# One token transfer of 256 KB in place of two of 128 KB in the spectral steps of a conv, attention and spectral-filter kernel

## The chip, the cores and the metric

The kernel runs on one core of one Trainium2 chip, as one launch. The metric is device microseconds for one execution; the time of a kernel is the median of several runs. A second figure, the span, is the time from the first to the last instruction of the one execution that the hardware profiler recorded.

## The reference, cut to what matters

The network has two images of 64 x 64 pixels and 128 channels (4096 tokens of 128 channels each). It normalises them, runs a convolutional self-attention block with four heads, then an attention of the tokens with themselves, and last a spectral layer. The change touches the spectral layer alone: a causal convolution of the tokens with 16 filters, each result multiplied by its own 128 x 128 matrix and summed.

```python
def _stu_conv(phi, u, n):
    Vf = jnp.fft.rfft(phi, n=n, axis=0)
    Uf_p = jnp.fft.rfft(u, n=n, axis=1)
    Uf_m = jnp.fft.rfft(u * sgn3, n=n, axis=1)
    U_plus = jnp.fft.irfft(Vf[None, :, :, None] * Uf_p[:, :, None, :], n=n, axis=1)[:, :sl]
    U_minus = jnp.fft.irfft(Vf[None, :, :, None] * Uf_m[:, :, None, :], n=n, axis=1)[:, :sl]
...
out = jnp.einsum('btkd,k,kde->bte', U_plus, s, Mpp)
out = out + jnp.einsum('btkd,k,kde->bte', U_minus, s, Mpm)
```

Here `btkd` are batch, time, filter and channel; the input is (2, 4096, 128) and there are K = 16 filters.

## The kernel before, in words

Up to about 1713 us the kernel does the first attention block, the second attention, and the preparation of the spectral layer. In that preparation the function `feed` transforms the tokens along one time index and writes them to DRAM as `rows16[b]`: float16, indexed by half (high and low part of the number), component, row, frequency and channel. The filters' tables lie in DRAM as `tables16`.

From there on the spectral layer runs in 64 steps, numbered by batch `b`, output parity `ro`, one of eight chunks of 16 frequencies `ch`, and stream `s`. A step has three parts.

- `fetch16(n)` brings the data of step `n` into SBUF. It is called for step `n + 2` at the head of step `n`. For each half of the chunk (8 frequencies) it issues two token transfers from GpSimd (L1213) and one table transfer of 1 MB from SyncE (L1222). A token transfer fills 64 partitions, one for each combination of half, component (2 x 2) and row (16), with one contiguous row of 8 frequencies x 128 channels, 2 KB. The two copies put the same data on partitions 0 to 63 and 64 to 127. In DRAM the source is a pattern of 4 blocks of 16 rows.
- `convolve16` multiplies on TensorE: 16 matmuls (L1606) with the tokens as weights and the tables as the moving operand, four for each of four windows `w`; windows 0 and 1 use the first half, 2 and 3 the second. ScalarE (L1613) and VectorE (L1614) split each result into two float16 parts.
- `mix16` multiplies these parts by the filters' matrices on TensorE, 48 matmuls (L1622). They are given out twelve at a time between the windows of the next step's `convolve16`.

The tiles have three turns: step `n` uses turn `n % 3` of `tokens_in` (a pair of tiles for each turn, one for each half) and of `tables_in` (the same). A fetch into a turn waits until the matmuls that read the old contents are done. The transfers and the spectral matmuls keep the order in which they are written (`ordered`). On the GpSimd queue a transfer also waits until the one eight places ahead of it has landed, because eight semaphores are used in turn there.

Other work goes beside the steps: `back` takes a finished quarter of the output, adds `base`, which it reads from DRAM with a transfer of 1 MB (`had`), and writes the result; in the first steps the rest of `feed` for the second batch is also on the GpSimd queue (`rows`, L1412 and L1413).

Of the kernel before, what the change touches and what calls it, by code (L numbers as in the profile page):

```python
# [13 lines left out]
F16 = mybir.dt.float16  # L14
# [8 lines left out]
P = 128  # L23
B, C, HH, WW = 2, 128, 64, 64
# [15 lines left out]
BP = NI // 2  # L40
# [7 lines left out]
NS = NF // NCH // 2  # L48
# [28 lines left out]
def conv_attn_hybrid(ctx: ExitStack, tc: tile.TileContext, io):  # L77
    nc = tc.nc
# [31 lines left out]
    def pool(stack, name, bufs=1, **kw):  # L110
        return stack.enter_context(tc.tile_pool(name=name, bufs=bufs, reuse_waits="tile", **kw))
# [5 lines left out]
    def chain(*parts):  # L117
        for p in parts:
            yield from p
# [589 lines left out]
    rows16 = [dram.tile([2, 2, DROWS, NF, C], F16, name=f"rows16_{b}") for b in range(B)]  # L709
# [44 lines left out]
    def network(layer0, in_halves):  # L754
        with ExitStack() as st:
            layers(st, layer0, in_halves)

    def layers(st, layer0, in_halves):
# [3 lines left out]
        tokens = [pool(st, f"tok{b}", side="right") for b in range(B)]  # L762
# [223 lines left out]
        def transform(p):  # L986

            fw = p.tile([P, 4, NF], F32, name="fw", bufs=1)
            aside.dma_start(fw, io["fw"])
            return fw  # L990
# [3 lines left out]
        if not in_halves:  # L994
            tokens_in = ffw.tile([P, 2, 2, WC // 2, C], F32, name="tokens_in")
# [53 lines left out]
        def rest16(p, steps):  # L1049
            wbr, top = chosen[:2]  # L1050
            ends = p.tile([P, NBR, P], F32, name="ends")
            aside.dma_start(ends, io["ends"].partition_broadcast(P))
            mu_raw = p.tile([P, NBR, NU, C], F32, name="mu_raw")
            aside.dma_start(mu_raw, io["mu"].rearrange("i n d e -> d i n e"))
            aside.dma_start(gw, io["gw16"])
            yield from steps
            weighted_sum(mask, ends, top)
            yield
            weighted_sum(mu, mu_raw, wbr)
            yield  # L1060
            nc.vector.scalar_tensor_tensor(
                gw, gw, OUT_SCALE, mask.unsqueeze(1).to_broadcast([P, 2, P]), ALU.mult, ALU.mult
            )
            yield
# [128 lines left out]
        def ordered(instruction):  # L1193
            return tc.keep_in_program_order(instruction)
# [4 lines left out]
        if in_halves:  # L1199
            tables_in, tokens_in = [], []  # L1200

        def fetch16(n, pieces=1):

            if n >= len(STEPS):
                return
            b, ro, ch, s = STEPS[n]
            row = FIRST[STREAM[ro, s]]
            for half in range(2):
                w0 = 2 * NS * ch + NS * half
                tt, ut = halves16(n)[half]  # L1210
                for copy in range(2):
                    ordered(
                        nc.gpsimd.dma_start(  # L1213
                            ut[64 * copy : 64 * copy + 64],
                            rows16[b].rearrange("h c r w d -> (h c) r w d")[:, row : row + BP, w0 : w0 + NS, :],
                        )
                    )
                own = tables16[s, w0 // NS]
                size = BP // pieces
                for part in range(pieces):  # L1220
                    ordered(
                        nc.sync.dma_start(  # L1222
                            tt[:, part * size : part * size + size],
                            bass.AP(
                                tensor=own.tensor,
                                offset=own.offset + part * size * NS * 2 * NK,
                                ap=[[NDI * NS * 2 * NK, 8], [NS * 2 * NK, BP], [1, size * NS * 2 * NK]],
                            ),
                        )
                    )  # L1230
                    yield

        def spaced(steps):
            for _ in steps:
                for _ in range(3):
                    yield

        def halves16(n):
            return list(zip(tables_in[n % 3], tokens_in[n % 3]))

        def attend16(b, p, beside, closed, drain=True):

# [217 lines left out]
        with ExitStack() as l1:  # L1460
            p1 = pool(l1, "l1")
            if not in_halves:
                lo.append(p1.tile([P, L], F32R, name="lo"))
            with ExitStack() as part:
                p = pool(part, "l1_a")
                gate = [0]

                def second_parts(n):
                    if n < NQ and not in_halves:
                        low = p.tile([P, 2, 512], F32, tag="low", name=f"low{n}")  # L1470
                        nc.sync.dma_start(low, lows[n].rearrange("n p c -> p n c"))
                        copy = nc.vector.tensor_copy(loT[0][:, bass.ts(n, 512)], low[:, 0])
                        if n == 0:
                            tc.keep_in_program_order(copy)
                        nc.vector.tensor_copy(lo[0][:, bass.ts(n, 512)], low[:, 1])

                def ready(i):
                    second_parts(i + 1)

                second_parts(0)  # L1480
                fw = None if in_halves else transform(p1)

                def closed(j):
                    gate[0] = j + 1

                y = [None]

                def stage(i, n):
                    y[0] = p.tile([P, 512], F32, tag="y", name=f"y1_{i}")
                    return y[0]  # L1490

                stats = LayerStats(p1, tok[1], "a1")
                second = normalise(1, stats, stage, gate)
                if in_halves:
                    steps = chain(left, rest16(p, stats.steps()), second)
                else:
                    steps = chain(left, stats.steps(), filters(p, fw), matrices(p), second)
                (attend16(0, p1, steps, closed) if in_halves else attend(0, p1, steps, closed, ready))
            right0.close()
            if in_halves:  # L1500
                early = pool(middle, "early", side="right")
                tables_early = [early.tile([P, BP, NS, 2 * NK], F16, name=f"tables_e{n}") for n in range(2)]
                tokens_in = [
                    [early.tile([P, NS, C], F16, name=f"tokens{turn}_{n}") for n in range(2)] for turn in range(3)
                ]
                tables_in.append(tables_early)
                late_pool = pool(right1, "late", 2, side="right")
                fw = transform(late_pool)
                banked = [bank]
                fed_to = [0]  # L1510
            if in_halves:
                mxr, mxl = mixing
            else:
                mxr, mxl = (x[0].rearrange("p (k s c) -> p k s c", k=NK, s=2) for x in (hiT, loT))
            with ExitStack() as part:
                p = pool(part, "l1_b", 2)
                fed = LayerStats(ffw, tok[1], "f1")

                def closed(j):
                    fed.take(range(4 * j, 4 * j + 4))  # L1520
                    fed.close(range(4 * j, 4 * j + 4))
                    own = slice(2 * j, 2 * j + 2)
                    m = p.tile([P, 2, 2, C], F32, tag="m", name=f"m{j}")
                    aside.dma_start(m, mx[own].rearrange("k p s c -> p k s c"))
                    nc.vector.tensor_copy(mxr[:, own], m)
                    nc.vector.tensor_tensor(mxl[:, own], m, mxr[:, own], ALU.subtract)
                    if in_halves:
                        fed_to[0] = j + 1

                if in_halves:  # L1530
                    ahead = spaced(fetch16(0, 4))
                    feed_1 = feed(1, late_pool, lambda name: banked[0](name), fw, fed, fed_to)
                    beside = chain(feed(0, late_pool, bank, fw), by_turns(ahead, feed_1))
                    attend16(1, p1, beside, closed, drain=False)
                    for _ in ahead:
                        pass
                else:
                    attend(1, p1, feed(0, p, bank, fw), closed)
# [12 lines left out]
        else:  # L1551
            tables_in = [
                px.tile([P, 2, WC // 2, 2 * BP * NK], F32, tag=f"b{n}", name=f"tables_in{n}") for n in range(2)
            ]
# [385 lines left out]
```

## Time and profile before

| | before |
|---|---|
| median of 3 runs | 2728.48 us |
| the three runs | 2701.92, 2728.48, 2751.97 us |
| profiled execution, its own time | 2752.85 us |
| its span | 2751.0 us |
| mean granted TensorE clock | 0.980 |
| TensorE busy (matmul) | 2585.8 us, 94% of the span |
| token transfers | 256 of 128 KB, median 27.7 us from issue to landing |
| first and last spectral matmul that reads tokens | 1713.1 and 2714.4 us |

How to read it: the page names an instruction by its line, its engine, its operation and its tiles, written `out<-in`. "PE cv L1606" is a matmul of line 1606 into tile `cv`. A DMA is named by its tiles; its time to landing runs from the issue by its engine to the last of its semaphore updates. Idle time of an engine is put down to what ended it. PE is TensorE, PEld its weight load, DVE VectorE, ACT ScalarE, POOL GpSimd, SP SyncE; a small q after an engine is its queue.

### The profile page before, as it was taken

The numbers are of one execution on the slowest core, as the hardware profiler recorded it, in microseconds if no ns is written. First come the engines' busy times: TensorE is split into PE (matmuls) and PEld (weight loads), VectorE is DVE, ScalarE is ACT, GpSimd is POOL, SyncE is SP. The second block draws the span as 40 slices with busy tenths as digits, with TensorE's granted clock in tenths as the row PEclk, the third lists the DMA queues.
The fourth block names the chain that finished last, engine by engine and source line by source line (L and its number), as shares of the span: only waits on it lengthen the run. The fifth ranks groups of instructions, "written<-read, shape, count | busy, mean of one in ns | idle before, by whom it ended". The sixth has DMA issues, their size and how long they took to land.

```text
span 2751.0 us, 32520 instructions
## 1 busy us (share of the span) xinstructions
PE 2585.8 (94%) x11955; PEld 1277.3 (46%) x11955; DVE 1671.0 (61%) x2946; ACT 1840.3 (67%) x2059; POOL 492.9 (18%) x792
## 2 busy tenths in 40 slices
PE   5999999999998989999989999988898989999998
PEld 3555555555544444444434444433353435445444
DVE  5256464246357426878876677756565656666664
ACT  4999999999998887666544554544454545555553
POOL 2022021012122401000233322311111111111110
PEclk9999999999999999999989999999999999999999
DMA  5122220012113504766366865665565666665661
GB/s 145 35 66 66 61 72 20 5 53 66 30 32 100 79 20 90 129 113 110 71 131 124 150 124 118 199 170 142 171 176 151 137 172 217 190 203 180 159 198 56
DMA packets 328874, 311.65 MB, mean 113 GB/s; under 512 B 276240, under 2 KB 278944, under 8 KB 312512
## 3 DMA queue, kind: packets, MB, share of 16 engines
q1 hardware_dynamic: 270480, 221.61, 31.6%
q0 software_dynamic: 56784, 85.44, 13.3%
q10 hardware_dynamic: 1440, 2.43, 0.3%
q8 instruction: 96, 1.57, 0.2%
q14 instruction: 74, 0.61, 0.1%
HBM read 212.27 MB, written 23.33 MB: 86 GB/s over the span
## 4 chain that ended last, share of the span: by engine, by line
PE 33%; DMA 13%; DVE 6%; issue 5%; ACT 1%; POOL 1%; SPq 0%; DVEq 0%; POOLq 0%; ACTq 0%
PE m L1622 17%; DMA tokens<-rows 10%; PE cv L1606 6%; PE od L1280 3%; PE oa L1280 3%; PE y L1252 3%; DMA eT<-pair 2%; DVE pair L1266 2%; DVE x L1614 1%; DVE both L1300 1%; PE bk L1740 1%; PE pf L1406 1%; ACT ey L1261 1%; PE ar L1388 1%; PE vt L1730 0%
## 5 line engine op out<-in xcount | busy, mean ns | idle before, releaser
L465 ACT ACTIVATE e<-s 128x1536 f16<-128x1536 f32 (+1 forms) x704 | 938.9, 1425 | 63.3 <-PE s L209 58.7
L1614 DVE TENSOR_TENSOR x<-cv,x 128x1024 f16<-128x1024 f32 x512 | 602.9, 1219 | 329.7 <-ACT x L1613 329.6
L1613 ACT CAST x<-cv 128x1024 f16<-128x1024 f32 x512 | 493.8, 1016 | 446.4 <-PE cv L1606 444.6
L1622 PE MATMUL m<-x,mxr 128*128 128x512 f16 x2048 | 624.4, 382 | 0.0
L209 PE MATMUL acc<-e,v 128*97 128x512 f16 x2048 | 562.1, 382 | 15.7 <-DVE accs L413 13.1
L209 PE MATMUL s<-qs,ks 128*128 128x512 f16 x2048 | 561.7, 382 | 7.3 <-ACT e L465 3.8
L1622 PE MATMUL m<-x,mxl 128*128 128x512 f16 x1024 | 393.5, 384 | 1.2 <-DVE oh L1629 1.2
L209 PEld LDWEIGHTS <-v 128*97 128x97 bf16 x2048 | 256.3, 125 | 230.4 <-issue 30.4
L1261 ACT ACTIVATE ey<-y,nshift 128x512 f32<-128x512 f32 x288 | 196.3, 688 | 195.3 <-PE y L1252 162.2
L1622 PEld LDWEIGHTS <-mxr 128*128 128x128 f16 x2048 | 201.7, 98 | 244.7 <-issue 7.4
L209 PEld LDWEIGHTS <-ks 128*128 128x128 f16 x2048 | 201.7, 100 | 230.8 <-issue 49.1
L1213 POOL DMA_DIRECT2D tokens<-rows x256 | 157.1, 614 | 742.7 <-DMA tokens<-rows 492.8
L1252 PE MATMUL y<-bothT 128*128 128x512 f16 x864 | 204.4, 383 | 3.1 <-ACT ey L1261 2.1
L1266 DVE TENSOR_TENSOR pair<-ey,pair 128x1024 f16<-128x1024 f32 x144 | 174.5, 1218 | 35.7 <-ACT pair L1265 35.1
L1280 PE MATMUL od<-pair,hi 128*128 128x512 f16 x576 | 185.3, 383 | 9.3 <-DVE oT L1292 5.8
L1300 DVE SCALAR_TENSOR_TENSOR both<-eT 128x512 f16<-128x512 f16 x224 | 153.7, 686 | 55.7 <-DMA eT<-pair 52.4
L1606 PEld LDWEIGHTS <-tokens 128*128 128x128 f16 x1024 | 98.6, 98 | 179.8 <-issue 49.8
L413 DVE COPY accs<-acc 97x512 f32<-97x512 f32 x64 | 44.1, 690 | 212.7 <-PE acc L209 212.6
L1622 PEld LDWEIGHTS <-mxl 128*128 128x128 f16 x1024 | 101.4, 99 | 128.9 <-issue 6.8
L1280 PEld LDWEIGHTS <-hi 128*128 128x128 f16 x1024 | 101.1, 99 | 125.6 <-issue 12.9
L1265 ACT CAST pair<-ey 128x1024 f16<-128x1024 f32 x144 | 150.6, 1046 | 4.6 <-DMA eT<-pair 2.2
L1280 PE MATMUL oa<-eT,hi 128*128 128x512 f16 x448 | 143.3, 381 | 0.0
(224 smaller groups left out, 2348.0 us busy)
## 6 DMA issues: line engine op xcount, KB each, us to landing
tables_a<-tables SPq DMA_DIRECT2D x42, 1024.0 KB
tables_b<-tables SPq DMA_DIRECT2D x42, 1024.0 KB
tables_e<-tables SPq DMA_DIRECT2D x42, 1024.0 KB
tokens<-rows POOLq DMA_DIRECT2D x256, 128.0 KB, 27.7
tab<-in_rot SPq DMA_DIRECT2D x32, 512.0 KB
rows<-uh POOLq DMA_DIRECT2D x128, 64.0 KB, 4.3
ks<-term POOLq DMA_DIRECT2D x112, 64.0 KB, 2.3
qs<-term POOLq DMA_DIRECT2D x112, 64.0 KB, 2.0
```

Of the source, the lines that this page charges most:

```text
L209: tc.keep_in_program_order(nc.tensor.matmul(*args, **kw))
L465: nc.scalar.activation(e[:, own, :], ps[:, own, :], AF.Exp, scale=SCORE_SCALE)
L1213: nc.gpsimd.dma_start(ut[64 * copy : 64 * copy + 64], rows16[b].rearrange("h c r w d -> (h c) r w d")[:, row : row + BP, w0 : w0 + NS, :],)
L1252: nc.tensor.matmul(ps[:, q, :], a[0][:, bass.ts(t, P)], c[0][:, bass.ts(i, 512)], start=(n == 0), stop=(n == 2),)
L1261: nc.scalar.activation(e[:, q, :], ps[:, q, :], AF.Exp, bias=nshift16, accum_out=den[:, t, i : i + 1])
L1266: nc.vector.tensor_tensor(pair[:, 1, own], e, pair[:, 0, own], ALU.subtract)
L1280: nc.tensor.matmul(acc, a[0][:, own], pair(m, t), start=(start and t == 0 and n == 0), stop=(stop and t == 3 and n == 2),)
L1300: nc.vector.scalar_tensor_tensor(both, eT[:, 0, :, u, :], 1.0, eT[:, 1, :, u, :], ALU.mult, ALU.add, accum_out=den[:, 4 * i + u, j : j + 1],)
L1606: ordered(nc.tensor.matmul(pu[:, h, :], ut[:, at, :], tt[:, :, at, :], start=True, stop=True))
L1613: nc.scalar.copy(hi, pur)
L1614: nc.vector.tensor_tensor(lo, pur, hi, ALU.subtract)
L1622: nc.tensor.matmul(acc, m, x, start=(s == 0 and i == 0), stop=(s == 1 and i == len(products) - 1))
```

## The change

The tokens of a step become one tile per turn, 16 frequencies wide (4 KB on each partition), and are brought by two transfers of 256 KB in place of four of 128 KB. The two copies on the partitions' halves remain. `halves16` hands out the two halves of the one tile as views, so the matmuls are the same. The two token transfers stand ahead of both table transfers of the step.

```diff
@@ fetch16
             row = FIRST[STREAM[ro, s]]
+            for copy in range(2):
+                ordered(
+                    nc.gpsimd.dma_start(
+                        tokens_in[n % 3][64 * copy : 64 * copy + 64],
+                        rows16[b].rearrange("h c r w d -> (h c) r w d")[
+                            :, row : row + BP, 2 * NS * ch : 2 * NS * ch + 2 * NS, :
+                        ],
+                    )
+                )
             for half in range(2):
                 w0 = 2 * NS * ch + NS * half
-                tt, ut = halves16(n)[half]
-                for copy in range(2):
-                    ordered(
-                        nc.gpsimd.dma_start(
-                            ut[64 * copy : 64 * copy + 64],
-                            rows16[b].rearrange("h c r w d -> (h c) r w d")[:, row : row + BP, w0 : w0 + NS, :],
-                        )
-                    )
+                tt = tables_in[n % 3][half]
                 own = tables16[s, w0 // NS]
...
         def halves16(n):
-            return list(zip(tables_in[n % 3], tokens_in[n % 3]))
+            return [(tt, tokens_in[n % 3][:, NS * h : NS * h + NS]) for h, tt in enumerate(tables_in[n % 3])]
...
                 tokens_in = [
-                    [early.tile([P, NS, C], F16, name=f"tokens{turn}_{n}") for n in range(2)] for turn in range(3)
+                    early.tile([P, 2 * NS, C], F16, name=f"tokens{turn}") for turn in range(3)
                 ]
```

## The prediction, made before the changed kernel ran

> **What bounds the kernel now.** I read the time first: the shown runs are 2701.92, 2728.48 and 2751.97 us. The profiled execution is one of the long ones: 2752.85 us with a span of 2751.0, so 1.85 us lie outside the span and it is 24.4 us above the median. Two per cent, about what a measurement of this kernel can tell from no change, is 55 us.
>
> Next the page. TensorE is busy for 94% of the span; then the chain, which names the transfer that the change touches:
>
> ```profile
> PE 2585.8 (94%) x11955; PEld 1277.3 (46%) x11955; DVE 1671.0 (61%) x2946; ACT 1840.3 (67%) x2059; POOL 492.9 (18%) x792
> ...
> PE 33%; DMA 13%; DVE 6%; issue 5%; ACT 1%; POOL 1%; SPq 0%; DVEq 0%; POOLq 0%; ACTq 0%
> PE m L1622 17%; DMA tokens<-rows 10%; PE cv L1606 6%; PE od L1280 3%; PE oa L1280 3%; PE y L1252 3%; DMA eT<-pair 2%; DVE pair L1266 2%; DVE x L1614 1%; DVE both L1300 1%; PE bk L1740 1%; PE pf L1406 1%; ACT ey L1261 1%; PE ar L1388 1%; PE vt L1730 0%
> ...
> tokens<-rows POOLq DMA_DIRECT2D x256, 128.0 KB, 27.7
> ```
>
> Ten per cent of the chain, some 289 us, is spent in flight of token transfers: 128 KB take 27.7 us to land. That is not what can be won, since the chain follows a transfer while TensorE works as well. What TensorE really loses is in the table by stretches; its columns are start and end, length, busy us (instructions) of PE, PEld, DVE, ACT and POOL, granted clock, DMA share, GB/s:
>
> ```profile
> 1713.00:1796.00 83.00, 78.86 (x331) 36.11 (x330) 59.95 (x86) 42.76 (x49) 30.88 (x46) 0.98 0.63 198
> 1796.00:1968.00 172.00, 147.71 (x645) 63.72 (x644) 96.58 (x84) 78.77 (x84) 25.54 (x41) 0.94 0.61 154
> 1968.00:2046.00 78.00, 77.51 (x399) 40.72 (x398) 53.43 (x48) 40.45 (x44) 12.99 (x22) 1.00 0.60 187
> 2046.00:2246.00 200.00, 175.08 (x786) 77.66 (x785) 115.92 (x101) 94.53 (x100) 29.33 (x47) 0.95 0.60 148
> ...
> 2354.00:2494.00 140.00, 139.02 (x642) 62.47 (x643) 96.05 (x84) 78.15 (x83) 25.10 (x41) 1.00 0.60 199
> ```
>
> So the 64 spectral steps have two starved stretches, 1796 to 1968 and 2046 to 2246. TensorE is idle 24.3 + 24.9 us there, and the clock that falls after each idle time costs 0.06 x 172 + 0.05 x 200 = 20 us more: 69 us is all that the tokens can give back in this execution. In the quick stretches a step takes 13.81 us (2118.84 to 2132.66 in the timeline), which is TensorE's own work. The waits, and the timeline where one ends, say who is late:
>
> ```profile
> PE cv L1606 <- DMA tokens<-rows: 20.1, 5, 11.5
> ...
> POOL tokens L1213 <- DMA tokens<-rows: 491.0, 160, 6.1
> POOL tokens L1213 <- PE cv L1606: 171.2, 40, 6.6
> ```
>
> ```profile
> 2102.48 1.89 PE L1606 MATMUL cv<-tables_b,tokens 128*128 128x512 f16 x4 [11.47 <-DMA tokens<-rows]
> ...
> 2116.72 1.22 POOL L1213 DMA_DIRECT2D tokens<-rows  x2 [5.57 <-PE cv L1606]
> ...
> 2118.84 1.03 PE L1606 MATMUL cv<-tables_e,tokens 128*128 128x512 f16 x4
> ...
> 2132.66 1.03 PE L1606 MATMUL cv<-tables_a,tokens 128*128 128x512 f16 x4
> ```
>
> POOL's 491 us are waits of a token transfer for the one eight transfers earlier on the same queue: at most eight are in flight, two steps' worth.
>
> **Why 128 KB take 27.7 us.** The trace's semaphore updates give it. Of the 16 increments of one token transfer eight come after 1.7 to 5.5 us and eight after 16 to 41 us. The packet records show why: table packets (8192 B) fly on at most eight engines at a time, and these eight are always occupied. Each token transfer leaves 32 packets of 4096 B, 16 semaphore writes of 4 B and 96 records of 8 B. If four engines carry data (8 packets each) the other twelve get 8 small fillers each, 12 x 8 = 96. So on every engine a token transfer is 8 packets and a semaphore write, 9 items, and on the eight table engines the items come out one for one with table packets (at 2126 us a filler each 0.63 us, behind a table packet of 0.63 us; in quick stretches behind one of 0.31).
>
> [...]
>
> **The change, part by part.**
>
> Issues: 128 fewer on POOL at 0.61 us, 78 us of POOL. POOL waits most of the time in this stage, so nothing on the path. TensorE, VectorE, ScalarE and SP keep their order.
>
> Queue limit: eight transfers are now four steps' worth and three buffers hold six, so the 491 us of POOL waits end. What limits the issue next is the buffer, that is `cv` on TensorE. By itself it is worth nothing, since the table engines' queue was never empty with eight in flight.
>
> Items: a row is now 4 KB, one packet. 16 packets (or fillers; I assume one for each packet as before) and one semaphore write make 17 items, two transfers a step: 34 in place of 4 x 9 = 36. The bytes are the same. In the starved stretches the token queue sets the pace, so 372 us x 2/36 = 20.7 us come back. The unknown here is the fillers. Lower bound of the cost: if they stay 8 per transfer, an engine has (17 + 3 x 9)/4 = 11 items a transfer, 22 a step. Upper bound: a row goes as two packets, 32 + 1 items a transfer and 66 a step, which I all but exclude, since the tables' rows of 8 KB go as one packet. I take 34.
>
> Deadline: before, the first half's tokens were due at the step's first `cv` and the second half's 6.9 us later; now the whole is due at the first. Likewise the buffer comes free as a whole at the last `cv`, three quarters into the step. Lead for the first half falls from 2.75 steps (38 us) to 2.25 (31 us). Where the queue sets the pace this costs at most 6.9 us once for a stretch, not for each step, since then transfer follows transfer: 13.8 us for two. In the quick stretch between them tokens gain more of a cushion: there 36 items took 13.5 us by the landings (0.375 each), so 34 take 12.8 against TensorE's 13.81; over the five steps 15 to 19 that is 3.5 us more than before. Net cost 10 us.
>
> Sum for the profiled execution: -20.7 + 10.3 = -10.4 us, so 2742.5 from 2752.85. The median run has 24.4 us less of stall, 45 of 69; the same share of the gain is 7 us: 2728.5 - 7 = 2721 us.
>
> **Rivals.**
>
> Nothing to see: landing is set by semaphore writes behind table packets whatever the transfer's size, and gain and cost cancel. For it: the two numbers are of one size. 2728 us.
>
> Tokens stop being the bound: fillers stay 8, 22 items a step. Then the tables are next. By the packet records they landed 19 us early at the end of the first starved stretch and 11 us at the end of the second, so 30 us of idle go and, at 20 us of clock to 49 of idle, 12 more: 42 in the profiled run, 27 in the median one: 2701 us. Against it: data packets and fillers were equal in number before.
>
> Slower: the one piece comes too late. Its place is the first `cv` of a step; its price is the landing less the lead. In quick stretches landings of 26 to 28 us fit into 31. In some 26 steps (5 to 14, 20 to 31, 37, 38, 52, 53; table packets take 0.45 us or more in most of them) landings are some 36 us; if the queue gets no faster, each waits 5 us where it now loses 69/26 = 2.7: 26 x 2.3 = 60 us, 2788 us. It decides from a landing of 31 us on. Against it: a paced queue costs the half step once.
>
> **How the numbers follow.** Forecast 0.42, nothing to see 0.20, tokens no longer the bound 0.18, slower 0.20. The range takes in most of both sides, 2688 to 2775; before's own runs spread over 50 us. Faster by over 2% (under 2674) would need nearly all 69 us gone: 0.05. Slower by over 2% (over 2783) is most of the last rival: 0.13. Within: 0.82.
>
> **What would show it.** Right: 128 token issues; POOL no longer waiting for token transfers; fillers of 4 B, 192 a transfer; landings of 25 to 35 us; starved stretches still there, at step starts alone, with some 60 us of idle and clock loss. Wrong: 96 fillers, landings under 15 us and no idle before `cv` (the second rival), or idle before the first `cv` of most steps (the last one).

## The result: 1% slower, and the profile after

| | before | after |
|---|---|---|
| median of 22 runs each, same chip | 2712.12 us | 2741.38 us |
| lowest and highest | 2689.75, 2758.07 | 2708.42, 2787.98 |
| profiled execution, its own time | 2752.85 us | 2726.16 us |
| its span | 2751.0 us | 2724.2 us |

The ratio after to before is 1.0096, with a 95% interval of 1.0069 to 1.0123: 26 us (0.0096 x 2712) more, where I had forecast 7 us less. Runs over 1.5% above the fastest of the same kernel are left out of this ratio and of all later ones. The two profiled executions must not be subtracted: the one of before is among its longest and the one of after is below its median. What they do show is which waits there are.

The page of after, its rows for busy time, the chain by engine, POOL's issues and the transfers (us to landing last):

```profile
PE 2578.6 (95%) x11955; PEld 1276.3 (47%) x11955; DVE 1670.5 (61%) x2946; ACT 1839.1 (68%) x2059; POOL 411.7 (15%) x664
...
q0 software_dynamic: 54736, 85.33, 13.7%
...
PE 41%; DVE 7%; issue 5%; DMA 5%; ACT 2%; POOL 1%; SPq 0%; DVEq 0%; POOLq 0%; ACTq 0%
...
L1210 POOL DMA_DIRECT2D tokens<-rows x128 | 77.1, 607 | 780.5 <-PE cv L1608 739.5
...
tokens<-rows POOLq DMA_DIRECT2D x128, 256.0 KB, 21.4
```

POOL is 81 us less busy, its 491 us of waits for older token transfers are gone, and a transfer lands 6 us sooner. The queue has 2048 packets less than the 56784 before: 64 steps x 32, which is 4 x (32 + 16 + 96) less 2 x (64 + 16 + 192). So the fillers are 192 a transfer, as assumed. TensorE still starves. The table by stretches (start and end, length, busy of PE, PEld, DVE, ACT, POOL, clock, DMA share, GB/s) and the waits of TensorE and POOL from 1690 us on:

```profile
1800.00:1900.00 100.00, 81.10 (x348) 35.04 (x347) 52.91 (x46) 41.74 (x44) 6.74 (x12) 0.91 0.60 146
1900.00:2200.00 300.00, 293.93 (x1399) 138.72 (x1398) 200.57 (x175) 161.49 (x173) 25.14 (x41) 0.99 0.62 187
2200.00:2400.00 200.00, 194.56 (x936) 93.85 (x934) 132.95 (x129) 104.38 (x112) 16.80 (x27) 0.98 0.63 189
2400.00:2600.00 200.00, 193.21 (x921) 92.94 (x920) 130.31 (x115) 102.40 (x111) 15.53 (x26) 0.97 0.62 164
```

```profile
PE cv L1608 <- issue: 35.1, 8, 9.1
...
POOL tokens L1210 <- PE cv L1608: 739.5, 55, 24.7
```

The 35.1 us before `cv` are put down to "issue", because the profile names no event at the very end of the wait. The semaphore updates do: the last one of the step's second token transfer comes 0.1 us before each of these matmuls. All stand at the first `cv` of a step, as the timeline shows (start, length, matmul, idle time before it in brackets):

```profile
1806.07 1.86 PE L1608 MATMUL cv<-tables_e,tokens 128*128 128x512 f16 x4 [4.21 <-issue]
...
1830.58 1.87 PE L1608 MATMUL cv<-tables_a,tokens 128*128 128x512 f16 x4 [9.14 <-issue]
...
1894.48 1.87 PE L1608 MATMUL cv<-tables_b,tokens 128*128 128x512 f16 x4 [4.68 <-issue]
...
1915.26 1.86 PE L1608 MATMUL cv<-tables_e,tokens 128*128 128x512 f16 x4 [5.25 <-issue]
```

So the waits stand at steps 6, 7, 11, 12, 40, 55 and 56 (and 0.2 us at 58), in three groups. In these seven steps the second transfer took 32.8 to 42.3 us to land. From the first `cv` of step 0 to that of step 63 this execution takes 970.2 us (1706.0 to 2676.2); the fastest versions below take 919 to 921.

### The profile page after: what moved, and what is told of

Same layout as the page of the kernel before. It is cut to its first block, busy times and chain, and to the rows that moved or that the text cites. A ratio compares the mean times of both kernels' runs of the same rounds, so it can differ in the third digit from the quotient of the medians.

```text
span 2724.2 us, 32269 instructions
## 1 busy us (share of the span) xinstructions
PE 2578.6 (95%) x11955; PEld 1276.3 (47%) x11955; DVE 1670.5 (61%) x2946; ACT 1839.1 (68%) x2059; POOL 411.7 (15%) x664
## 4 chain that ended last, share of the span: by engine, by line
PE 41%; DVE 7%; issue 5%; DMA 5%; ACT 2%; POOL 1%; SPq 0%; DVEq 0%; POOLq 0%; ACTq 0%
PE m L1624 22%; PE cv L1608 7%; PE oa L1282 3%; PE od L1282 3%; PE y L1254 3%; DMA eT<-pair 2%; DVE pair L1268 2%; DVE x L1616 1%; DMA tokens<-rows 1%; DVE both L1302 1%; PE bk L1742 1%; DMA base<-oc 1%; DMA rows<-uh 1%; ACT ey L1263 1%; PE pf L1408 1%
## 5 line engine op out<-in xcount | busy, mean ns | idle before, releaser
L209 PE MATMUL acc<-e,v 128*97 128x512 f16 x2048 | 561.0, 381 | 16.4 <-DVE accs L413 13.8
L209 PEld LDWEIGHTS <-v 128*97 128x97 bf16 x2048 | 256.2, 125 | 230.6 <-issue 30.4
L1210 POOL DMA_DIRECT2D tokens<-rows x128 | 77.1, 607 | 780.5 <-PE cv L1608 739.5
## 6 DMA issues: line engine op xcount, KB each, us to landing
tokens<-rows POOLq DMA_DIRECT2D x128, 256.0 KB, 21.4
```

Source lines behind the costliest of these rows:

```text
L209: tc.keep_in_program_order(nc.tensor.matmul(*args, **kw))
```

## The experiments

Each ratio is to the kernel before, run beside it on the same chip. Where a difference of two ratios is given, its half width is the root of the sum of the squares of theirs.

### The deadline or the release

The change moves two things for the half that is used second: it is due a half step earlier, and the buffer comes free for both halves together. The first run has before's four transfers, in reversed order, so that POOL waits for the second half's buffer first and the second half is in front:

```diff
-            for half in range(2):
+            for half in (1, 0):
...
```

> The kernel before, with its four transfers of 128 KB, but the second half's two are issued ahead of the first half's. So the issue of all four waits for the last matmul on the old tile, and the first matmul of a step waits for all four: release and deadline of the change, without its transfer size. Theory D (the one piece is released and due as a whole, half a step worse on both ends): slower than before as the change is, ratio 1.01, up to 1.017 since 36 items a step remain. Theory S (the 256 KB transfers themselves, 16 packets in a row on four engines): no difference from before, 1.000.

Measured: 1.0119 [1.0029, 1.0209]. It loses about what the changed kernel loses, without its transfer size. A repeat narrowed this:

> The kernel with four transfers, the second half's first, once more, for a narrower interval. It has the change's release and deadline with 36 items a step instead of 34. If two items are worth what the prediction gave them (20.7 us, 0.8%), its ratio is 1.0096 + 0.008 = 1.017 or more. If the deadline alone makes the change's loss and two items are worth nothing, it is 1.0096 like the change, inside 1.007 to 1.012.

Measured: 1.0104 [1.0066, 1.0142]. The next run keeps before's deadlines and delays the release alone:

```diff
-            for half in range(2):
+            if n > 2:
+                ordered(nc.gpsimd.memset(halves16(n)[1][1][:, 0, :2], 0.0))
+            for half in (0, 1):
...
```

> The kernel before with its four transfers of 128 KB in its own order, but GpSimd may issue the first of them only once both halves of the turn are free (a small write into the second half's tile stands ahead of them). So the release is as late as with the change, while the second half is still due 6.9 us after the first. If the deadline (the whole step due at its first matmul) is what costs, the time is as before: ratio 1.000, at most 1.004. If the late release is what costs, it is as with the change: 1.008 to 1.012, some 22 to 33 us, with TensorE idle at the first cv of the steps in the starved stretches. A third outcome, halfway (1.005), would mean that both count.

Measured: 1.0018 [0.9981, 1.0055]. The waits of TensorE in the repeat and, second, with the late release:

```profile
PE cv L1609 <- DMA tokens<-rows: 35.7, 8, 11.6
PE cv L1609 <- issue: 19.9, 7, 8.6
```

```profile
PE cv L1611 <- issue: 13.4, 3, 11.1
PE cv L1611 <- DMA tokens<-rows: 10.2, 4, 5.3
```

The late release costs 0.2%, not distinguishable from nothing; the earlier deadline costs the rest, 0.0104 - 0.0018 = 0.0086 with a half width of 0.005, some 23 us. Why the late release costs so little can be seen in before: in its steps 41 to 47, which do not wait, a step's first transfer is issued only 30.4 to 31.3 us ahead of its first `cv`, some 0.5 us after the transfer eight places ahead has landed. The limit of eight had taken the half step of lead already; the changed kernel has 29.8 to 30.1 us in steps 43 to 47. In the same steps of before the second half's tokens land 3.9 to 5.1 us after the first `cv`: in time for a use 6.9 us after it, and late for the new deadline. The opposite edit, an earlier issue with the deadline left whole, gave seven half slots in one tile to the changed kernel, so that a fetch starts 2.75 steps ahead again:

```diff
-                    early.tile([P, 2 * NS, C], F16, name=f"tokens{turn}") for turn in range(3)
+                tokens_in = [early.tile([P, 7 * NS, C], F16, name="tokens")]
...
```

> The changed kernel with its 256 KB transfers, but the tokens lie in a ring of seven half-step slots in place of six (2 KB more on each partition), and step n+3's transfer is issued as soon as the first half of step n is used: lead 2.75 steps (38 us) in place of 2.25 (31 us). One step in seven wraps and takes four transfers. Theory D: the loss goes, ratio 0.99 to 1.00. Theory S: stays at 1.01.

Measured: 1.0143 [1.0062, 1.0223]; landings went from 21.4 to 32.2 us. The fetches were issued 36.7 to 37.0 us ahead in quick steps, so the half step was given to the transfers, and it went into longer landings. As I read it, a step's tokens are held up by what is in the queue, not by when they are issued. One step in seven has four transfers here, so the queue holds a little more as well.

### What the queue is short of

The 192 fillers of a transfer are 12 x 16, and its 64 packets of 4096 B are 4 x 16. I read this as data on four engines at a time, as many as the source has blocks; whether the one follows from the other is not shown by these two kernels. The same bytes in 64 KB pieces, each one block of 16 rows:

```diff
             for copy in range(2):
+                for block in range(4):
...
-                        tokens_in[n % 3][64 * copy : 64 * copy + 64],
+                        tokens_in[n % 3][at : at + BP],
```

> The changed kernel with each of the two transfers split in four of 64 KB, one block of 16 rows each[...]. On a table engine a step is then 8 data packets and 8 semaphore writes, 16 items in place of 34, with the same bytes. Theory Q (the number of items in turn with table packets sets the tokens' pace): landing under 15 us, nearly no starved stretch, ratio 0.98 to 0.99. If the bytes on the table engines set the pace, or the release as a whole: 1.00 to 1.01.

Measured: 0.9915 [0.9887, 0.9943], landing 8.8 us. Eight transfers a step in place of two, and it is faster than both kernels. As an estimate, a piece is 16 packets of 4096 B and 16 semaphore writes, as many writes as a transfer of before or after has; spread evenly over 16 engines that is 2 items from each piece, 16 a step in place of 34. Where the data of this run fell is not shown. Then the same by another order of the partitions (row first), in two transfers of 256 KB; the tables, in the same order, go in pieces of 512 KB:

```diff
-                        rows16[b].rearrange("h c r w d -> (h c) r w d")[...],
+                        bass.AP(tensor=src.tensor, offset=src.offset,
+                                ap=[[NF * C, BP], [DROWS * NF * C, 4], [1, 2 * NS * C]]),
...
-                                ap=[[NDI * NS * 2 * NK, 8], [NS * 2 * NK, BP], [1, size * NS * 2 * NK]],
+                                ap=[[NS * 2 * NK, 16], [NDI * NS * 2 * NK, 4], [1, size * NS * 2 * NK]],
```

> The changed kernel with partitions in the order copy, row, block for tokens and tables alike (the sum over partitions is the same). Then [...]two token transfers of 256 KB on 16 engines (4 packets and a semaphore write on each engine, 10 items a step), and four table transfers of 512 KB on 16 engines in place of two of 1 MB on eight. All theories that put the stall in the eight table engines: stall gone, about 60 us less than the changed kernel, ratio 0.975 to 0.985. If TensorE's starved stretches have another cause: 1.01.

Measured: 0.9899 [0.9847, 0.9950], landing 7.2 us, no wait of TensorE for a transfer in the stage. This run changes the tables' transfers as well as the tokens'; the one before it leaves the tables as they are. The 16 increments show the difference. For token transfers, the times in us from issue to each of the 16 updates, sorted, with the start of the transfer in front:

```
after    2105.7  1.7 1.7 1.7 1.8 7.4 8.1 8.2 8.7 16.1 17.4 17.5 17.7 18.0 18.4 19.5 20.3
after    2119.5  1.7 1.7 1.7 1.7 1.7 1.7 1.8 1.8 10.7 14.1 14.4 15.0 16.9 18.6 20.4 22.7
perm16   2100.3  5.2 5.2 5.2 5.2 5.3 5.3 5.3 5.3 5.4 5.4 5.5 5.5 5.5 5.5 5.5 5.6
```

In the row of perm16 all sixteen updates stand within 0.4 us, where those of after have eight early and eight late. I read this as data spread over all 16 engines, the tables' too; the DMA share of the last version below, 0.84 and 0.86 against 0.62 and 0.63 in the changed kernel, fits that. Landing is 21.4 us in the changed kernel against 7.2 for the same 256 KB here, and 8.8 for 64 KB with the tables unchanged.

### Do the stretches start with had?

A transfer of 1 MB into `had` stands in the token queue three times, in the changed kernel during steps 4, 20 and 36 (1786, 2043 and 2276 us). It was moved to SyncE's queue, first in before, then in after:

```diff
-                    aside.dma_start(whole, baser[:, ro])
+                    nc.sync.dma_start(whole, baser[:, ro])
```

> The kernel before with the 1 MB transfer of base into had on SyncE's queue, with the tables, instead of GpSimd's, with the tokens. Starved stretches began after each of the three had transfers and in the first quarter. If had, standing in the token queue, starts them, they go except the first quarter's: 30 to 40 us less, ratio 0.985 to 0.990. If the tables' share of the engines starts them, had on their queue starts them just as well: ratio 1.00.

> The changed kernel with had on SyncE's queue. If the change's loss is the earlier deadline, once for each starved stretch that had starts, its loss against the kernel before with the same edit shrinks from 26 us to what the first quarter's stretch costs, about 7 us (0.25%); in ratios to the kernel before 0.988 to 0.993 if the edit takes those stretches away. If the loss comes from every step and not from stretches, the distance between the two stays about 1%.

Measured: before with it 0.9868 [0.9819, 0.9917], after with it 0.9896 [0.9861, 0.9931]. So `had` starts them, the first quarter's too: the profile of the former has no wait for tokens left. One line gives before 1.3%. The distance between the two is 0.0028, half width 0.006; with a repeat of the latter further down (0.9929) it is 0.004, half width 0.006. The latter's profiled execution, 2716.24 us, is the longest of its 14. TensorE waits 22.9 us for tables in it, and the 5.9 us of "issue" are tokens: they stand before steps 58, 60 and 62, where the second transfer lands 0.1 us ahead:

```profile
PE cv L1608 <- DMA tables_b<-tables: 14.8, 3, 9.4
PE cv L1608 <- issue: 5.9, 3, 2.4
PE cv L1608 <- DMA tables_e<-tables: 5.1, 2, 4.9
PE cv L1608 <- DMA tables_a<-tables: 3.0, 2, 2.8
```

Then without the three transfers at all; zeros take their place, so three quarters of the output lack `base`:

```diff
-                    aside.dma_start(whole, baser[:, ro])
+                    nc.vector.memset(whole, 0.0)
```

> The kernel before without the three transfers of base into had; a write of zeros by VectorE[...] stands in their place, so three quarters of the output lack base. If had in the token queue starts the starved stretches, all of the loss goes except what the last quarter's own base transfers start: ratio 0.985 to 0.988, as with had on SyncE's queue (0.987). If the first quarter's stretch comes from the token writes of the second batch instead, 30 us stay and the ratio is about 0.997.

> The same edit in the changed kernel, again without base in three quarters of the output. If the change loses only in the stretches that had starts, it now stands within 0.2% of the kernel before with this edit. If it loses in the ordinary steps too, or at each burst of 4 KB packets, the distance stays at 0.3 to 1%, and the trace shows idle time of TensorE before cv by tokens or by tables in steps without had.

Measured: 0.9866 [0.9805, 0.9928] and 0.9972 [0.9939, 1.0004], a distance of 0.0106 with a half width of 0.007. The medians of the two, 2688.83 and 2703.89 us on one chip, lie 15 us or 0.6% apart, so the lower part of that range is the likelier. Either way my theory of that moment, that the change loses only where `had` starts a stretch, fell. The timeline of the changed kernel without `had` shows waits at the starts of even steps (10, 12 and 14 here; the second line is step 11's first `cv`, which has none):

```profile
1871.02 1.02 PE L1608 MATMUL cv<-tables_a,tokens 128*128 128x512 f16 x4 [3.41 <-issue]
...
1884.83 1.03 PE L1608 MATMUL cv<-tables_b,tokens 128*128 128x512 f16 x4
...
1902.50 1.18 PE L1608 MATMUL cv<-tables_e,tokens 128*128 128x512 f16 x4 [3.32 <-issue]
...
1933.26 1.02 PE L1608 MATMUL cv<-tables_b,tokens 128*128 128x512 f16 x4 [1.28 <-DVE x L1616]
```

There the second token transfer lands 0.1 us before the even steps 8, 10, 12 and 14, and 2.4 to 3.6 us ahead of the odd steps 9 to 15. In before without `had`, whose profile has no wait for tokens, the same steps have the tokens of their first half 4 to 20 us before the first `cv`.

### What an item costs

Two transfers of 1 KB a step that nobody reads, then one:

```diff
             for copy in range(2):
+                ordered(
+                    nc.gpsimd.dma_start(
+                        more[copy][n % 3], rows16[b][0, 0, row : row + BP, 2 * NS * ch, :32]
+                    )
+                )
```

> The changed kernel with two more transfers of 1 KB a step on GpSimd's queue[...], which nobody reads: 38 items a step on a table engine instead of 34, with 0.4% more bytes. The prediction priced an item by its number alone: at 0.375 us each 38 take 14.25 us a step, more than TensorE's 13.81, so all steps would be starved: 64 x 0.44 = 28 us, and the starved stretches 4/34 longer; ratio to the kernel before 1.02 or more against the change's 1.0096. If what counts is the packets that carry data and the table packets between them[...]: 1.010 to 1.013.

> The changed kernel with one more transfer of 1 KB a step[...], which nobody reads: 36 items a step instead of 34, like the kernel before, the rotation and the deadlines as with the change, and eight transfers in flight are still more than the buffers allow. With four items more (two such transfers) the ratio rose from 1.010 to 1.030. If the number of items does that, two items cost half of it: 1.018 to 1.022. If the limit of eight in flight, which two such transfers reach, did it, 1.010 to 1.013.

Measured: 1.0296 [1.0219, 1.0374] with two, 1.0202 [1.0095, 1.0310] with one. Above the changed kernel's 1.0096 that is 0.020 (half width 0.008) for four items and 0.011 (half width 0.011) for two, some 14 us an item, if an added transfer is two items on each engine, which no run shows. But this is not the price of an item, because the added transfers also made tokens late. The profile with one, its waits and its timeline of GpSimd before step 16:

```profile
POOL more L1210 <- DMA more<-rows: 86.5, 4, 27.2
```

```profile
1925.67 0.51 POOL L1210 DMA_DIRECT2D more<-rows  x1
1953.37 0.50 POOL L1210 DMA_DIRECT2D more<-rows  x1 [27.19 <-DMA more<-rows]
1953.88 1.24 POOL L1216 DMA_DIRECT2D tokens<-rows  x2
```

GpSimd stands for 27 us until an added transfer (`more`) has landed, and the tokens of step 16 stand behind it. The same happens at steps 32 and 48. The tokens of these three steps are issued 15 to 16 us after their buffer is free, in the changed kernel within 1.5 us. TensorE then waits 5.8, 11.1 and 6.1 us at these steps, where the changed kernel's profile has no wait: 23 of the 31 us by which its waits for transfers exceed that profile's. With two added transfers the same steps are hit. The limit of eight is reached too, against what I expected: with one added transfer, eight were in flight at 39 of 187 issues. So what an item costs by itself stays open.

### Where the data falls

Four transfers with 36 items and the change's deadline (1.0104) should have been 0.5% slower than the changed kernel with 34 (1.0096) by the prediction's price. They are 0.0008 slower, half width 0.005: a gain isn't seen, and isn't quite excluded. If there is one, something may give it back. The increments name a candidate. In after, from 1750 to 2650 us, table packets of 8192 B fly eight or fewer at a time in 98% of the time, so I count eight table engines. A row of eight early updates that are all at 1.7 to 1.8 us (2119.5 above) I read as eight engines that had only fillers, with the data on engines that carry tables; one of four at 1.7 to 1.8 and four at 7.4 to 8.7 us (2105.7) as data off them. In the changed kernel the first is so for both transfers of the even steps (eighth update mostly by 2.2 us) and for neither of the odd ones (at 7 to 11 us); in before, in every step, for the two of the first half (mostly by 2.2 us, against 4 to 6 for the second half's).

> The changed kernel with one more transfer, of 256 bytes on four partitions, on GpSimd's queue ahead of step 3's tokens, and nothing else. By the semaphore updates the data of successive token transfers goes to four engines, then the next four, with period four: with two transfers a step, both fall on the engines that carry tables in even steps and neither in odd ones; with four a step, two of them in each step. The added transfer moves the rotation by one, so that each step has one on table engines and one off. If this bunching is part of the loss, as large as two items saved, the ratio to the kernel before falls from 1.0096 to about 1.000, and TensorE's idle time no longer comes in every second step. If the deadline alone makes the loss, the ratio stays at 1.0096.

> The same with two added transfers of 256 bytes: the rotation moves by two, the bunching stays and only odd steps take the place of even ones. Both theories say 1.0096 here, inside 1.006 to 1.014; if it falls like the run with one added transfer, the added transfer acts in some other way than by the rotation.

> The changed kernel with the rotation moved by one and had on SyncE's queue. With had there the kernel before stood at 0.987 and the changed one at 0.990, in whose profile TensorE waited for tables. If the bunching of token packets on the table engines also made those tables late, it is now 0.985 to 0.987 with no idle time before cv. If not, 0.990.

The edits add one or two issues at step 3:

```diff
+            for extra in range(1 if n == 3 else 0):
+                ordered(nc.gpsimd.dma_start(more[extra], rows16[b][0, 0, row : row + 4, 2 * NS * ch, :32]))
```

Measured: 1.0062 [1.0004, 1.0121], 1.0106 [1.0073, 1.0140] and 0.9929 [0.9890, 0.9969]. By the updates of all three traces the data still fell on table engines in even steps, so a transfer of 256 bytes did not move the groups, and these runs do not test the idea. They are repeats of the changed kernel (with `had` on SyncE's queue in the third, whose profile has no wait for tables). A transfer of 128 KB did move them, and two moved them back:

```diff
+            if n == 2:
+                ordered(
+                    nc.gpsimd.dma_start(
+                        more[0],
+                        rows16[b].rearrange("h c r w d -> (h c) r w d")[
+                            :, row : row + BP, 2 * NS * ch : 2 * NS * ch + NS, :
+                        ],
+                    )
+                )
```

> The changed kernel with one more transfer of 128 KB, shaped like a token transfer of the kernel before, ahead of step 2's tokens, 200 us before step 2 runs; nobody reads it. In the traces the transfers of 256 bytes did not move the rotation of the four-engine groups: both transfers of every even step still fell on table engines. In the run with seven half slots, steps with four transfers of 128 KB moved it by four places, so transfers of this size count. If this one moves it by one, each step has one transfer on table engines. Then, if the bunching is part of the loss, the ratio falls from 1.010 to 1.000 to 1.004, and TensorE's idle time no longer keeps to alternate steps. If the deadline alone makes the loss, it stays at 1.007 to 1.013. If the semaphore updates show both transfers of even steps on table engines as before, the groups do not follow a count of transfers, and nothing follows on bunching.

> The changed kernel with two added transfers of 128 KB ahead of step 2's tokens, on the two halves of the partitions. One such transfer moved the rotation by one place, so that in every step one of the two transfers fell on table engines, and the ratio rose from 1.010 to 1.024, against what I expected of it. With two the rotation moves by two places, and both transfers of every second step fall on table engines again. If the place of the groups made turn1 slower, the ratio is back at 1.007 to 1.013. If the added transfer itself did it, by its bytes or by its place on the queue, it is 1.024 or more.

Measured: one gives 1.0237 [1.0189, 1.0285], two give 1.0101 [1.0065, 1.0138]. The updates show the even steps' pair on table engines again with two, and one of each step's two with one:

```
turn1    1978.0  1.7 1.7 1.7 1.7 7.2 7.5 8.3 8.8 15.9 16.0 16.4 19.2 20.9 21.1 22.5 25.2
turn1    1978.6  1.6 1.7 1.7 1.8 6.8 7.1 7.9 8.4 26.1 26.1 26.2 26.5 28.2 28.7 29.4 30.0
turn1    1992.2  1.7 1.7 1.7 1.7 1.7 1.7 1.8 1.8 17.6 17.7 19.3 21.7 22.8 25.6 26.7 26.7
turn1    1992.8  1.7 1.7 1.8 2.0 7.9 7.9 8.3 8.5 25.1 25.1 26.3 27.0 27.7 30.2 31.3 31.3
```

In the even step (1992) the first transfer's data is on table engines. In the odd one (1978) it is the second's, as I read it: its four updates at 6.8 to 8.4 us are those of the engines that still carry the first one's data.

The page's rows for the transfers, with one and then with two (the profiled execution with one, 2801.77 us, is 24 us above its median, so part of this difference can be that execution's own):

```profile
tokens<-rows POOLq DMA_DIRECT2D x128, 256.0 KB, 28.0
```

```profile
tokens<-rows POOLq DMA_DIRECT2D x128, 256.0 KB, 22.0
```

So which engines take the data, as I read the updates, is worth 0.0136 (half width 0.006), with transfers, bytes and deadlines of the stage the same; but in the other direction than I expected: one on and one off in each step lands later in all steps than both on, then both off. With one added transfer (turn1) the two groups of table engines carry data in different steps, so that in every step some of them are late; in the changed kernel all are late together and then recover together. That reading is argued from the updates, not tested. Whether before's arrangement, one pair of each step on table engines, is better or worse than these isn't tested either.

### The version that comes out of it

The permuted partitions and the one line for `had`, together:

```diff
+                                ap=[[NS * 2 * NK, 16], [NDI * NS * 2 * NK, 4], [1, size * NS * 2 * NK]],
...
+                    nc.sync.dma_start(whole, baser[:, ro])
```

> The kernel with tokens and tables on all 16 engines (ratio 0.990), and had on SyncE's queue as well (0.987 alone). Both left no idle time before cv in the profiled execution, so there is nothing left to add: 0.986 to 0.990, with TensorE's own work as the bound. If the two fix different executions, the longest runs come down and it is 0.983 or less.

Measured: 0.9810 [0.9750, 0.9870], lowest and highest 2674.79 and 2680.89. Its median, 2675.49 us against 2717.69, gives 0.9845. Its stretches in the spectral stage have a full clock and next to no idle TensorE:

```profile
1900.00:2200.00 300.00, 299.18 (x1433) 142.07 (x1432) 206.35 (x181) 164.81 (x176) 20.70 (x42) 1.00 0.84 186
2200.00:2400.00 200.00, 199.38 (x969) 96.27 (x967) 138.32 (x134) 109.48 (x117) 13.81 (x28) 1.00 0.86 195
```

What is left there is TensorE's own work. With `had` moved in before alone, or with the permuted partitions alone, the intervals overlap with this one, and the medians (2681.78 and 2678.57 us, on other chips) are within 7 us of it. So how much the second edit adds to the first stays open.

## Why the prediction was wrong, point by point

**The bound: right.** Tokens' landings starved TensorE in stretches, at step starts, and all of the loss could be given back there: the permuted partitions (0.9899), the 64 KB pieces (0.9915), or `had` out of the token queue (0.9868 in before) took it away.

**Issues and queue limit: as forecast.** 128 issues, 81 us less POOL, no wait for older transfers. That these are worth nothing by themselves fits the result; no run separates it.

**Items: the gain was not seen, and the price stays open.** I gave two items 20.7 us in the profiled execution, 13.5 in the median. With the same deadline, 34 items are only 2 us better than 36 (0.0008 x 2712, half width 13), so the 13.5 are neither seen nor quite excluded. The added transfers cannot settle the price, since they made tokens late. The prediction also left out the place of the data: it treated data packets and fillers as alike on every engine. That place was worth 1.4% between two arrangements. That it took the items' gain is not shown, and the one comparison speaks against it: with one transfer of each step on table engines, as before has one pair in each step, the changed kernel became slower and not faster.

The place could have been seen ahead. In before the updates have a period of four token transfers: those issued at 1994.6 and 1995.8 us have eight at 1.7 to 1.8 us, those at 1999.2 and 2001.5 have four by 2.4 us and four at 3.8 to 4.9, and at 2007.4 it begins anew. If the place goes by the count of such transfers, two a step alternate between even and odd steps. With one added transfer of 128 KB it moved by one place (turn1), which fits. Why the 256-byte transfers did not move it is not shown.

**Deadline: this is the step that failed.** I wrote that where the queue sets the pace it "costs at most 6.9 us once for a stretch, not for each step", and so 13.8 us less 3.5 of cushion for two stretches: 10.3 us, 7 in the median run. Measured by before's four transfers in reversed order, deadline and late release together cost 28 us (0.0104, half width 10), and the deadline 23 of them (half width 14). The term counted only stretches that starve in before. It put at nothing the steps that come through before with a few us to spare and fall short once the second half is due 6.9 us sooner: steps 41 to 47 of before have 1.8 to 3.0 us to spare there, and without `had`, where before does not wait for tokens at all, the changed kernel does and is 15 us slower by the medians. The stretches are also not two: the profile after has three groups of waits.

Whether a stretch pays the half step more than once is not shown. Three or four payments of 6.9 us, 21 to 28 us, would be the measured loss as well. In the repeat with reversed order TensorE waits at each of steps 10 to 16 (8.4 us at most, 17.8 in sum), which would fit several payments, but before's steps 12 to 16 wait too. The waits at steps 10, 12 and 14 without `had` fall on the steps whose data is on table engines, so they do not tell the deadline from the place of the data.

Of the 33 us between the forecast of -7 and the result of 26, the deadline with the release makes 21 (28 - 7), and the gain that was not seen the other 11 (13.5 - 2), which is within the noise.

**Landings.** I expected 25 to 35 us; the median was 21.4, from 7.9 to 42.3. The lead was as worked out, 29 to 31 us in quick steps; only the 38 us of before, from which I let it fall, were 30 to 31 in its own quick steps 41 to 47.

**The rivals.** The third one, that the one piece comes too late at the first `cv`, named the place and the mechanism: the waits are at the first `cv`, and the seven steps that waited had landings above its limit of 31 us. Its price of 60 us was too high, since landings fell and few steps waited. "Nothing to see" is excluded by the interval. Fillers did not stay at 8.

**Open.** What an item costs; whether the half step is paid more than once in a stretch; why the changed kernel starves at steps 54 to 56 without a `had` near; why seven half slots were no better than three turns; why tables came late in one execution with `had` on SyncE's queue.

## What to carry to other kernels

Before joining transfers, look in the trace at how many engines one of them uses and what else these engines carry: here two transfers of 256 KB, each on four engines by my count (64 packets of data, 192 fillers), cost 1%, and eight of 64 KB, which landed in 8.8 us in place of 21.4, saved 0.9%. A join moves the deadline of the last piece up to that of the first; look for the steps whose last piece has little time to spare, also where nothing waits yet. And look for the large transfer in the queue of the small ones: moving one line to another queue gave 1.3%.

## What the runs showed that I had not expected

- The increments of a transfer come in two groups: in the two rows shown of the changed kernel eight come within 8.7 us of the issue and the other eight after 10.7 to 22.7 us (256 KB), against all sixteen within 5.2 to 5.6 us in the row shown of perm16, with the order of the partitions changed for tokens and tables.
- A transfer of 1 KB that nobody reads, issued once a step, is not free: GpSimd stood 26 to 27 us for the landing of one at three steps, and the tokens behind it were 15 to 16 us late.
- One transfer of 128 KB, 200 us before the stage starts, made the kernel 1.4% slower than two such transfers did (1.0237 and 1.0101). The updates show, as I read them, that the engine groups of all later transfers had moved.
